# Cross-attention and expert feed-forward on one core: a written order for every stage, with the first feed-forward group prepared in the last attention units

## The chip, the cores and the metric

The kernel runs on one core of a Trainium2 chip. The metric is the device time of one execution in microseconds (us); lower is better. The time given for the kernel is the median of its runs. One execution is also recorded by the hardware profiler; all durations below come from that record. The engines are TensorE (PE, with its weight loads as PEld), VectorE (DVE), ScalarE (ACT), GpSimd (POOL) and SyncE (SP), which issues most of the DMAs.

## The reference

All data are float32. There are 32 sequences of 100 tokens, 512 features wide (3200 tokens), and a context of 722 rows for each, of which the causal mask leaves the first 100 visible.

```python
# attention, 16 heads of 32
q = layernorm(x) @ WQ.T;  k = ctx @ WK.T;  v = ctx @ WV.T
scores = einsum('bhqd,bhkd->bhqk', q, k) / sqrt(32)       # causal mask
y = einsum('bhqk,bhkd->bhqd', softmax(scores), v)
x = x + y @ Wfc.T + bfc
# feed-forward on h = layernorm(x): a shared expert and 16 routed ones, inner width 1024
shared = (gelu(h @ Ws_g.T) * (h @ Ws_u.T)) @ Ws_d.T       # all 3200 tokens
s = softmax(h @ gate_w.T)                                 # every token, 16 experts
w, idx = top_k(s, 12)                                     # 12 tokens of each sequence for each expert
eo = (gelu(h[idx] @ Wg.T) * (h[idx] @ Wu.T)) @ Wd.T * w   # 384 tokens per expert
x = x + shared + scatter_add(eo)
```

## The kernel before

Every float32 matrix product of a projection or of the feed-forward is made of three matmuls (`mm3`): each operand is split into a high half (a copy to fp32r on ACT) and a low half (the operand less its high half, on DVE or POOL), and high times high, high times low and low times high are added in PSUM.

**Attention** (`attention`) works in 32 units: a superblock `sb` of four sequences (400 tokens, `SB`) by a column block `c` of four heads. The K and V projections run over blocks of context rows (`KVB`: two blocks of 256 rows, then seven of 384); they go to DRAM and come back by unit (`kload`, `vload`). The first two blocks, the weights' splits and the first superblock of x are made in a prologue, whose order a scheduler chooses by a simulated timeline (`TCKW`). The units are in a list written by hand (`tc.manual_schedule()`): every engine, SP among them, takes its instructions in the written order. Unit `u` makes the q projection of `u` (`qproj`), scores and softmax of `u - 1`, and the transposed probabilities (`p_turn`, copied out of PSUM by `p_keep`) and products with V (`values`) of `u - 2`, so two further units drain the pipeline. The softmax is done in two halves: `sm_max` (DVE), `sm_sub` (POOL), `sm_exp` (ACT), `sm_sum` (DVE), `sm_mul` (POOL). From unit `KS` = 2 to unit 29 each unit makes one of four K projections of a block (`kproj`, kept by `kkeep`) and, in three of four units, one V projection (`vproj`). The x of the next superblock is normalised (`x_stats`, `x_norm` on DVE, the inverse root on POOL) and transposed on PE (`x_turn`), whose output shares two PSUM buffers, `ms`, with `p_turn` and `values`. In the unit, `x_norm` stands behind the second `sm_sum`:

```python
                if a is not None:
                    sm_sum(a, 1)
                    sm_mul(a, 1)
                if xs:
                    x_norm(sb + 1, c)
```

The result y of a unit goes to DRAM (`y_keep`, L291).

**Feed-forward** (`feed_forward`) has no written order. The scheduler places all its instructions, and its first ones among the last attention units. It loads and splits Wfc (L448 to L450, lower half on POOL), held back until the k load of unit `LATE` = 26 is issued (`issue_after`). The 25 tiles of 128 tokens form ten groups (`GROUPS`: five of two tiles, five of three). `prep` of a group loads y (`big<-yD`) and x, splits y, and for each tile makes y times Wfc on PE, adds bias and x, normalises, stores the normalised rows (`xnD`), transposes and splits them; then the router's logits. `ffn` runs over eight chunks of the inner width: 24 gate and up matmuls (`gu`) of as many columns as the group has tokens, gelu (ACT), product, split into `hh` and `hl`, and nine down matmuls (`dn`, for three tiles) one chunk later. Weights come as 768 KB chunks through two buffers (`wraw`) and are split by ACT (L435) and DVE (L436); the shared expert's chunks are split once and kept. `hook` prepares the next group after chunk 0; before the last group it also calls `route`, which takes the top 12 through DRAM and makes the slot lists. For each expert the rows are gathered by an indirect DMA on POOL, transposed, run through the same `ffn`, scaled, and added to the output by an indirect DMA (L610). While an expert runs, the scheduler splits the next expert's weights into the place of the chunks done.

Of the kernel before, what the change touches and what calls it, by code (L numbers as in the profile page):

```python
# [23 lines left out]
FB = dict(pre=2, r=7, raw=2, g=2, h=2)  # L24
# [3 lines left out]
KS = 2  # L28
LATE = 26
BUF = dict(cr=4, raw=5, cx=8, x=6, v=2, kk=2, kt=3, vt=2, q=3, p=5, pt=5, y=2, pj=2, sc=1, tr=2)  # L30
GROUPS = [2, 2, 2, 2, 2, 3, 3, 3, 3, 3]
# [28 lines left out]
def attention(tc, K):  # L60
    nc = tc.nc
    with ExitStack() as ctx:
        def pool(name, bufs, **kw):
            return ctx.enter_context(tc.tile_pool(name=name, bufs=bufs, **kw))

        xp = pool("a_x", BUF["x"])
        xnp = [pool("a_xn0", 1)]
        raw = pool("a_raw", BUF["raw"])
        crp = pool("a_cr", BUF["cr"])
        cxp = pool("a_cx", BUF["cx"])  # L70
        kkp = pool("a_kk", BUF["kk"])
        ktp = pool("a_kt", BUF["kt"])
        vtp = pool("a_vt", BUF["vt"])
        wpool = pool("a_w", 1)
        xnp.append(pool("a_xn1", 1))
        vp = pool("a_v", BUF["v"])
        qp = pool("a_q", BUF["q"])
        cst = pool("a_c", 1)
        stp = pool("a_st", 3)
        pp = pool("a_p", BUF["p"])  # L80
        ptp = pool("a_pt", BUF["pt"])
        yp = pool("a_y", BUF["y"])
        ps_kv = pool("a_kv", BUF["pj"], space=PSUM)
        ps_sc = pool("a_sc", BUF["sc"], space=PSUM)
# [5 lines left out]
        for w in range(3):  # L90
            WH.append(wpool.tile([128, NC4, D], FR, name=f"wh{w}"))
            WL.append(wpool.tile([128, NC4, D], FR, name=f"wl{w}"))
# [3 lines left out]
        def split(hi, lo, src):  # L96
            nc.scalar.copy(hi, src)
            nc.vector.tensor_tensor(lo, src, f32(hi), ALU.subtract)

        def load_w(w, dk):  # L100
            r = raw.tile([128, D], F32, name="raw")
            nc.sync.dma_start(r, K.wA[w, :, dk, :])
            split(WH[w][:, dk, :], WL[w][:, dk, :], r)

        def load_wc(w, c):
            r = raw.tile([128, D], F32, name="raw")
            rv = r.rearrange("p (d n) -> p d n", d=NC4)
            cs = slice(c * 128, (c + 1) * 128)
            nc.sync.dma_start(rv, K.wA[w, :, :, cs])
            split(WH[w][:, :, cs], WL[w][:, :, cs], rv)  # L110
# [43 lines left out]
        def x_turn(sb, b):  # L154
            xt = cur["x", sb, b]
            tp = ps_ms.tile([128, NC4, S], F32, name="ms")
            for dk in range(NC4):
                nc.tensor.transpose(tp[:, dk, :], xt[:, dk * 128:(dk + 1) * 128],  # L158
                                    K.ident[0:S, 0:S])
            cs = slice(b * S, (b + 1) * S)  # L160
            split(cur["xh", sb][:, :, cs], cur["xl", sb][:, :, cs], tp)
# [32 lines left out]
        def kload(u):  # L194
            sb, c = divmod(u, NC4)
            kt = ktp.tile([128, SB], F32, name="kt")
            cur["dma"] = nc.sync.dma_start(kt, K.kD[:, c, sb * SB:(sb + 1) * SB])
# [66 lines left out]
        def p_turn(u, b):  # L264
            p = cur["p", u, b // 2][0]
            tp = ps_ms.tile([128, NC4, S], F32, name="ms")
            for h in range(4):
                nc.tensor.transpose(tp[0:S, h, :], p[:, b % 2, h, :], K.ident[0:S, 0:S])  # L268
            cur["tp", u, b] = tp

        def p_keep(u, b):
            pt = ptp.tile([S, 4, S], F32, name="pt")
            nc.scalar.copy(pt, cur["tp", u, b][0:S])  # L273
            cur["pt", u, b] = pt

        def values(u):
            sb, c = divmod(u, NC4)
            ys = ps_ms.tile([128, NC4, S], F32, name="ms")
            for b in range(4):
                pt, v = cur["pt", u, b], cur["v", sb, b]  # L280
                for h in range(4):
                    d0 = c * 128 + 32 * h
                    nc.tensor.matmul(ys[32 * h:32 * h + 32, b, :], v[:, d0:d0 + 32],  # L283
# [3 lines left out]
        def y_keep(u):  # L287
            sb, c = divmod(u, NC4)
            y = yp.tile([128, SB], F32, name="y")
            nc.scalar.copy(y.rearrange("p (b s) -> p b s", b=4), cur["y", u])  # L290
            nc.sync.dma_start(K.yD[c, :, sb * SB:(sb + 1) * SB], y)  # L291

        nsb = K.nsb
        NU = nsb * NC4
        nc.gpsimd.dma_start(mask, K.mask)
        load_wc(0, 0)
        for d in range(NC4):
            ctx_load(0, d)
        for d in range(NC4):
            ctx_split(0, d, nc.vector)  # L300
        for c in range(1, NC4):
            load_wc(0, c)
        for dk in range(NC4):
            load_w(1, dk)
        for c in range(NC4):
            kkeep(0, c, kproj(0, c))
        for d in range(NC4):
            ctx_load(1, d)
        for d in range(NC4):
            ctx_split(1, d, nc.vector)  # L310
        for b in range(4):
            x_load(0, b)
            x_stats(0, b)
            x_norm(0, b)
        load_wc(2, 0)
        for i in range(KVB[0]):
            vkeep(0, i, vproj(0, i))
        for b in range(4):
            x_turn(0, b)
        for c in range(NC4):  # L320
            kkeep(1, c, kproj(1, c))
        for c in range(1, NC4):
            load_wc(2, c)
        for i in range(KVB[1]):
            vkeep(1, i, vproj(1, i))
        for d in range(2):
            ctx_load(2, d)
        for d in range(2):
            ctx_split(2, d)
        for d in range(2, NC4):  # L330
            ctx_load(2, d)
        x_load(1, 0)

        NU = nsb * NC4
        blocks = range(2, len(KVB))
        with tc.manual_schedule():
            for u in range(NU + 2):
                sb, c = divmod(u, NC4)
                mine, a, back = u < NU, u - 1, u - 2
                a = a if 0 <= a < NU else None  # L340
# [5 lines left out]
                jn, d = divmod(u + 2, NC4)  # L346
                jn += 2
                jl, dl = divmod(u + 4, NC4)
                jl += 2
                xs = mine and sb + 1 < nsb  # L350
                if mine:
# [391 lines left out]
```

## Time and profile before

| | |
|---|---|
| median of 3 runs | 1761.69 us (1761.47 to 1763.64) |
| profiled execution, its own time | 1757.8 us |
| its span, first to last instruction | 1756.0 us |
| mean granted clock of TensorE | 0.985 |
| busy: PE, DVE, ACT, POOL | 97%, 49%, 39%, 25% |
| DMA | 211.15 MB, mean 120 GB/s |

The busy shares are over the span. "Clock" is the share of TensorE's full clock that the chip granted. A line of a timeline gives start, duration, engine, source line, operation, output and input with their shapes, and in brackets how long the engine had stood before it and what released it. A line of the waits gives the waiting engine and line, what it waited for, and us in total, number of times and longest. Matmul records end by a model, so a busy PE is not always a PE at its peak.

### The profile page before, as it was taken

The numbers are of one execution on the slowest core, as the hardware profiler recorded it, in microseconds if no ns is written. First come the engines' busy times: TensorE is split into PE (matmuls) and PEld (weight loads), VectorE is DVE, ScalarE is ACT, GpSimd is POOL, SyncE is SP. The second block draws the span as 40 slices with busy tenths as digits, with TensorE's granted clock in tenths as the row PEclk, the third lists the DMA queues.
The fourth block names the chain that finished last, engine by engine and source line by source line (L and its number), as shares of the span: only waits on it lengthen the run. The fifth ranks groups of instructions, "written<-read, shape, count | busy, mean of one in ns | idle before, by whom it ended". The sixth has DMA issues, their size and how long they took to land.

```text
span 1756.0 us, 28445 instructions
## 1 busy us (share of the span) xinstructions
PE 1698.6 (97%) x11272; PEld 1560.4 (89%) x11272; DVE 854.9 (49%) x2131; ACT 685.8 (39%) x1100; POOL 440.8 (25%) x401
## 2 busy tenths in 40 slices
PE   7999999959999999999999999999999999999996
PEld 6888888848999999999989999999999999999996
DVE  5666666665334443333454444444444445444441
ACT  4455555544222221121243444444444444444431
POOL 2777777661100110011020111110111110011111
PEclk9999999979999999999999999999999999999998
DMA  7344444364111121101053555544555554454431
GB/s 234 102 130 130 137 131 132 119 206 137 55 55 58 64 66 43 37 31 49 28 193 134 161 162 157 149 141 147 162 162 150 156 160 134 156 155 136 142 90 18
DMA packets 83652, 211.15 MB, mean 120 GB/s; under 512 B 9569, under 2 KB 36434, under 8 KB 83520
## 3 DMA queue, kind: packets, MB, share of 16 engines
q1 hardware_dynamic: 72592, 184.07, 31.8%
q0 software_dynamic: 10784, 25.21, 7.4%
q8 instruction: 88, 1.44, 0.3%
q14 instruction: 44, 0.36, 0.1%
q10 hardware_dynamic: 144, 0.07, 0.0%
HBM read 163.71 MB, written 45.60 MB: 119 GB/s over the span
## 4 chain that ended last, share of the span: by engine, by line
PE 90%; DVE 2%; DMA 2%; ACT 2%; POOL 2%; issue 1%; SPq 0%; POOLq 0%; ACTq 0%; DVEq 0%
PE gu L55 46%; PE dn L55 23%; PE kv L55 10%; PE m L55 4%; PE ms L268 2%; PE sc L227 2%; PE ms L283 1%; PE m L595 1%; POOL p L247 1%; DVE p L238 1%; PE m L495 1%; PE ms L158 1%; PE m L504 1%; DMA r<-wA 0%; ACT p L251 0%
## 5 line engine op out<-in xcount | busy, mean ns | idle before, releaser
L55 PE MATMUL gu<-xh,whl 128*128 128x384 f32 (+1 forms) x3328 | 656.8, 327 | 0.1
L55 PEld LDWEIGHTS gu<-xh,whl 128*128 128x128 f32 x3328 | 561.8, 188 | 16.8 <-ACT g L542 0.3
L436 DVE TENSOR_TENSOR whl<-wraw,whl 128x1536 fp32r<-128x1536 f32 x136 | 240.8, 1771 | 279.6 <-ACT whl L435 277.7
L55 PE MATMUL dn<-whl,hh 128*128 128x512 f32 x1168 | 362.5, 395 | 0.0
L55 PE MATMUL gu<-xl,whl 128*128 128x384 f32 (+1 forms) x1664 | 345.3, 326 | 0.0
L55 PEld LDWEIGHTS gu<-xl,whl 128*128 128x128 f32 x1664 | 285.9, 188 | 2.3
L435 ACT CAST whl<-wraw 128x1536 fp32r<-128x1536 f32 x136 | 201.0, 1479 | 136.9 <-PE dn L55 128.2
L610 POOL DMA_INDIRECT out_dram<-r,isl x48 | 77.3, 1610 | 693.7 <-ACT r L609 683.9
L546 ACT CAST hh<-g 128x384 fp32r<-128x384 f32 (+1 forms) x208 | 102.4, 492 | 380.0 <-DVE g L543 379.0
L55 PEld LDWEIGHTS dn<-whl,hh 128*128 128x128 f32 x1168 | 214.3, 188 | 33.9
L55 PE MATMUL dn<-whl,hl 128*128 128x512 f32 x584 | 225.4, 395 | 0.0
L542 ACT ACTIVATE g<-gu 128x384 f32<-128x384 f32 (+1 forms) x208 | 97.8, 470 | 270.3 <-PE gu L55 251.3
L543 DVE TENSOR_TENSOR g<-g,gu 128x384 f32<-128x384 f32 (+1 forms) x208 | 109.4, 526 | 188.6 <-PE gu L55 187.5
L547 DVE TENSOR_TENSOR hl<-g,hh 128x384 fp32r<-128x384 f32 (+1 forms) x208 | 112.4, 540 | 102.6 <-ACT hh L546 102.6
L55 PEld LDWEIGHTS dn<-whl,hl 128*128 128x128 f32 x584 | 109.5, 188 | 25.5
L247 POOL TENSOR_TENSOR p<-p,mx 100x800 f32<-100x800 f32 x64 | 97.9, 1548 | 80.2 <-DVE mx L238 76.0
L238 DVE CUSTOM_DVE_ANT_0 p<-sc,mask 100x100 f32<-100x100 f32 x512 | 95.7, 257 | 22.7 <-PE sc L227 22.7
L262 POOL TENSOR_TENSOR p<-p,sm 100x800 f32<-100x800 f32 x64 | 101.9, 1593 | 8.0 <-DVE sm L257 7.0
L488 POOL TENSOR_SCALAR rs<-mv 128x1 f32<-128x1 f32 x25 | 6.9, 278 | 341.1 <-DVE mv L486 341.1
L256 DVE TENSOR_REDUCE sm<-p 100x8 f32<-100x800 f32 x64 | 63.1, 985 | 32.2 <-ACT p L251 32.2
L590 POOL DMA_INDIRECT big<-xnD,isl x48 | 51.3, 1069 | 95.7 <-DVE isl L673 61.3
L268 PE MATMUL ms<-ident,p 100*100 100x100 f32 x512 | 57.4, 257 | 11.4 <-ACT pt L273 7.8
(116 smaller groups left out, 1659.8 us busy)
## 6 DMA issues: line engine op xcount, KB each, us to landing
wraw<-wE SPq DMA_DIRECT2D x136, 768.0 KB
xt<-x SPq DMA_DIRECT2D x32, 200.0 KB
vD<-vt SPq DMA_DIRECT2D x25, 256.0 KB
kt<-kD SPq DMA_DIRECT2D x32, 200.0 KB
v<-vD SPq DMA_DIRECT2D x8, 800.0 KB
yD<-y SPq DMA_DIRECT2D x32, 200.0 KB
r<-x SPq DMA_DIRECT2D x25, 256.0 KB
xnD<-r SPq DMA_DIRECT2D x25, 256.0 KB
```

The source lines that it names most:

```text
L55: r = nc.tensor.matmul(out, t[0][a], t[1][b], start=(first and i == 0), stop=(last and i == n - 1))
L238: nc.vector.tensor_tensor_reduce(out=p[:, bb, h, :], in0=sc[:, h, cs], in1=mask, scale=ISCALE, scalar=NEG, op0=ALU.add, op1=ALU.max, accum ...
L247: nc.gpsimd.tensor_tensor(pv, pv, mx[:, :, None].to_broadcast([S, 8, S]), ALU.subtract)
L262: nc.gpsimd.tensor_tensor(pv, pv, sm[:, :, None].to_broadcast([S, 8, S]), ALU.mult)
L268: nc.tensor.transpose(tp[0:S, h, :], p[:, b % 2, h, :], K.ident[0:S, 0:S])
L435: nc.scalar.copy(h, r)
L436: nc.vector.tensor_tensor(l, r, f32(h), ALU.subtract)
L542: nc.scalar.activation(g[:, 0:n], pg[:, 0:n], AF.Gelu)
L543: nc.vector.tensor_tensor(g[:, 0:n], g[:, 0:n], pu[:, 0:n], ALU.mult)
L546: nc.scalar.copy(hh[:, 0:n], g[:, 0:n])
L547: nc.vector.tensor_tensor(hl[:, 0:n], g[:, 0:n], f32(hh[:, 0:n]), ALU.subtract)
L610: ins = nc.gpsimd.indirect_dma_start(out=K.out, out_offset=bass.IndirectOffsetOnAxis(ap=isl[:, i:i + 1], axis=0), in_=o, in_offset=None, c ...
```

## The change

All stages get a written order. For PE, ACT, DVE and SP it holds to the end; POOL keeps its written order in attention, and the scheduler places its instructions after that.

- The prologue is a list of steps (`prologue`), with loads apart from splits. The lower halves of three of the four WQ column blocks are made on POOL. `KS` is 1, so K and V projections run in units 1 to 28, and V of the second block moves partly into unit 0. `x_norm` moves ahead of the second `sm_sum`.
- Wfc is loaded and split in units 9 to 12 (`FC_AT`), lower half on DVE; the other constants follow in unit 13.
- The pools of the K and V path close after unit 28, and the feed-forward's buffers open in their place. The first group (now three tiles) is prepared in units 29 to 31 and the drain after them: y and x loads at the end of unit 28, bias, `split_y`, `fc` and so on between the attention steps (`end` is 0 in unit 29, -1 in unit 28); the first two weight chunks are loaded in unit 29 and split in thirds or whole. Gate and up of chunk 0 (`begin`) stand before the last unit's `p_turn`.
- The feed-forward is a class whose `job` runs eight chunks; after each chunk's gate, up and `hidden` come the steps listed in `mid[f]`, then the down products of the chunk before, then the steps listed in `post[f]`. Preparation of the next group, routing, gathers, `gturn` (transposes of gathered rows) and weight splits are placed by these lists.
- There are nine groups instead of ten. Attention's x buffers are 5 instead of 6, its raw buffers 6 instead of 5; transposed tiles in PSUM are laid out 128 apart instead of 100.

The core of the diff:

```diff
-KS = 2
-LATE = 26
-GROUPS = [2, 2, 2, 2, 2, 3, 3, 3, 3, 3]
+KS = 1
+FC_AT = 9
+GROUPS = [3, 2, 2, 3, 3, 3, 3, 3, 3]
...
+                if FC_AT <= u < FC_AT + NC4:
+                    fr = load_w(3, u - FC_AT)
+                if u == FC_AT + NC4:
+                    F.load_consts()
+                if end == 0:
+                    F.chunk_load()
+                    F.chunk_load()
+                if end == 1:
+                    pr.add(0)
+                    pr.stats(0)
+                    pr.rsqrt(0)
+                if end == 2:
+                    pr.add(2)
+                    pr.stats(2)
+                    pr.rsqrt(1)
+                    pr.store(0)
                 if a is not None:
                     scores(a)
...
                 if a is not None:
                     sm_exp(a, 0)
+                if end == 0:
+                    pr.split_y(0)
                 if back is not None:
                     p_turn(back, 0)
                     p_turn(back, 1)
                     p_keep(back, 0)
                     p_keep(back, 1)
...
+                if end == 1:
+                    pr.fc(1)
+                    pr.norm(0)
+                    F.chunk_split(0, 0)
+                if end == 2:
+                    pr.turn(0)
+                    pr.norm(2)
...
+                if xs:
+                    x_norm(sb + 1, c)
                 if a is not None:
                     sm_sum(a, 1)
                     sm_mul(a, 1)
-                if xs:
-                    x_norm(sb + 1, c)
...
+                if end == 0:
+                    pr.fc(0)
+                if end == 1:
+                    pr.fc(2)
+                if end == 2:
+                    F.chunk_split(0, 1)
+                    pr.turn(1)
                 if back is not None:
                     values(back)
+                if end == -1:
+                    kvctx.close()
+                    F.open_first()
...
+                    pr.load_y()
+                    for i in range(pr.nt):
+                        pr.load_x(i)
...
+    def job(self, e, xh, xl, nt, sink, mid, post):
+        acc = []
+        for f in range(NFC):
...
+                parts = self.gate_up(e * NFC + f, xh, xl, nt)
+            for p in mid.get(f, []):
+                p()
+            self.down()
+            self.pend = acc, f, nt, sink, parts
+            for p in post.get(f, []):
+                p()
...
+            if g == 0:
+                for f in range(NFC - 2):
+                    at(post, f, lambda f=f: self.chunk_split(f + 2))
+            if g + 1 < ng:
+                p = self.prep(g + 1)
+                at(post, 0, p.load_y, *[lambda i=i: p.load_x(i) for i in range(p.nt)])
+                at(post, 1, *[lambda i=i: p.bias(i) for i in range(p.nt)])
+                at(post, 1, p.split_y)
+                for i in range(p.nt):
+                    at(mid, 2 + i, lambda p=p, i=i: p.fc(i))
+                    at(post, 2 + i, lambda p=p, i=i: p.ln(i))
+                    at(post, 3 + i, lambda p=p, i=i: p.store(i))
+                    at(mid, 4 + i, lambda p=p, i=i: p.turn(i))
+                at(mid, 7, p.logits)
+                at(post, 7, p.tokens)
+            if g == ng - 1:
+                r = Route(self)
+                at(mid, 0, lambda: r.turn(0, 12))
+                at(mid, 1, lambda: r.turn(12, 12), lambda: r.turn(24, 1))
+                at(post, 1, r.load)
+                at(post, 2, *[lambda j=j: r.top(j) for j in range(4)], r.exchange)
+                at(mid, 4, r.slots)
+                at(post, 4, lambda: self.gather(0, r))
+                for i in range(NST):
+                    at(mid, 7, lambda i=i: self.gturn(0, i))
+                for f in range(1, NFC):
+                    at(post, f, lambda f=f: self.chunk_split(NFC + f - 1))
...
+            if g + 2 == ng:
+                Route.softmax(self)
...
+        for e in range(self.K.ne):
+            mid, post = {}, {}
+            if e + 1 < self.K.ne:
+                at(post, 0, lambda: self.gather(e + 1, r))
+                for i in range(NST):
+                    at(mid, 3 + i, lambda i=i: self.gturn(e + 1, i))
+                at(post, 0, lambda: self.chunk_split(NFC * (e + 2) - 1))
+                for f in range(1, NFC):
+                    at(post, f, lambda f=f: self.chunk_split(NFC * (e + 2) + f - 1))
```

Weight chunks still pass through two raw buffers: each finished split asks for the next load (`chunk_load`). After unit 31 the drain is written out in this order: scores and `sm_max` of the last unit, `p_turn` of the one before, `turn(2)`, `values`, the halves of the last softmax with the logits and the last third of chunk 0 between them, chunk 1's split, gate and up of chunk 0, `tokens`, then `p_turn`, `values` and `y_keep` of the last unit.

## The prediction

> **What bounds the kernel now.** I read the page first, then a table of windows cut where TensorE (PE) changes its behaviour, then the waits of PE, then the timeline at the waits.
>
> ```profile
> PE 1698.6 (97%) x11272; PEld 1560.4 (89%) x11272; DVE 854.9 (49%) x2131; ACT 685.8 (39%) x1100; POOL 440.8 (25%) x401
> ...
> PEclk9999999979999999999999999999999999999998
> ```
>
> PE is busy for 97% of 1756.0 us, so no other engine bounds the whole; what can be won is the 57 us in which PE stands, and whatever it works at a reduced clock. The windows (columns: PE, PEld, DVE, ACT, POOL busy us with instruction counts, clock, DMA share, GB/s) say where:
>
> ```profile
> 0.00:45.00 45.00, 34.40 (x220) 30.04 (x220) 24.50 (x77) 21.58 (x45) 12.77 (x22) 1.00 0.75 233
> 45.00:60.00 15.00, 12.97 (x100) 11.74 (x104) 8.82 (x43) 5.88 (x13) 11.99 (x11) 0.77 0.12 42
> 60.00:345.00 285.00, 274.94 (x3142) 248.76 (x3137) 188.99 (x1071) 153.63 (x311) 204.79 (x181) 0.98 0.43 129
> 345.00:400.00 55.00, 36.65 (x408) 30.63 (x407) 33.60 (x128) 28.19 (x46) 35.24 (x25) 0.78 0.60 194
> 400.00:900.00 500.00, 499.64 (x2931) 455.59 (x2930) 208.81 (x379) 113.30 (x210) 55.10 (x74) 1.00 0.19 62
> 900.00:925.00 25.00, 22.73 (x129) 20.57 (x128) 14.87 (x18) 11.00 (x16) 4.12 (x4) 1.00 0.60 209
> 925.00:1742.20 817.20, 817.20 (x4359) 763.10 (x4357) 375.26 (x418) 351.53 (x464) 112.55 (x85) 1.00 0.48 141
> 1742.20:1756.00 13.80, 0.01 (x1) 0.00 (x0) 0.00 (x0) 0.72 (x2) 4.27 (x3) 0.62 0.47 57
> ```
>
> The feed-forward stage (400 to 1742) has no idle PE but 2.3 us at 900 to 925. The losses lie in attention and at its end (345 to 400: 18.3 us idle). PE's own waits name them:
>
> ```profile
> PE ms L158 <- DVE xt L152: 15.4, 7, 5.3
> PE ms L268 <- ACT pt L273: 7.8, 1, 7.8
> ```
>
> The first is seven waits of `x_turn` for `x_norm`: one of 5.3 us at 41.7, where units 0 and 1 have no K and V projection, and six of 1.68 us, one in each unit with no V projection. There DVE does `sm_sum` first and the norm after it (normed at 90.07, PE turns at 90.71):
>
> ```profile
> 88.93 0.99 DVE L256 TENSOR_REDUCE sm<-p 100x8 f32<-100x800 f32 x1 [0.32 <-ACT p L251]
> 89.95 0.20 DVE L257 RECIPROCAL sm<-sm 100x8 f32<-100x8 f32 x1
> 90.07 0.50 DVE L152 TENSOR_SCALAR xt<-xt,mv,rs 100x512 f32<-100x512 f32 x1
> ```
>
> The 7.8 us wait is an ACT copy behind the Wfc conversion, whose load comes late:
>
> ```profile
> 356.06 1.29 ACT L449 CAST wfh<-r 128x512 fp32r<-128x512 f32 x2 [6.95 <-DMA r<-wA]
> ```
>
> The clock costs more. Two pairs of windows, each with a wait for `x_norm` in its first:
>
> ```profile
> 130.94:134.35 3.41, 1.73 (x50) 1.32 (x51) 2.07 (x4) 2.23 (x7) 3.39 (x3) 1.00 0.44 112
> 134.35:137.77 3.42, 3.42 (x39) 3.22 (x32) 2.28 (x24) 0.36 (x1) 1.12 (x2) 0.50 0.89 232
> ...
> 260.62:264.03 3.41, 1.96 (x64) 1.72 (x68) 1.84 (x4) 2.19 (x6) 3.39 (x3) 1.00 0.49 139
> 264.03:267.50 3.47, 3.47 (x38) 3.32 (x31) 3.11 (x33) 0.49 (x1) 1.65 (x2) 1.00 0.88 227
> ```
>
> With 1.73 us busy of 3.41 the next 3.42 us run at half clock; with 1.96 they do not. This happens at 134, 220 and 305. The Trainium skill ("TensorE: Matmul & The Clock Gate", section "Why this matters for your kernels") has the clock fall after one whole idle window, and allows gaps up to about 3 us. By it the 1.68 us gaps cost only themselves and the change wins nothing on the clock here (a sum of -23.7 below, 1738); by the rows each half-clock window costs 3.41/2 = 1.7 us more, three times 5.1 us (-28.8, 1733). The measured rows decide, and I follow them.
>
> **The change part by part** (minus is a gain, in us of PE's path, against the profiled 1756.0 span and its 1757.8 run).
>
> 1. *Start of the units* (KS 2 to 1). Unit 1 now has a K projection (12 x 0.174 = 2.1) and a V projection (12 x 0.234 = 2.8) between its q projection and `x_turn`: 4.9 us of work, plus the earlier norm, against the 5.3 us wait. It goes, and with it the half clock behind it (0.77 in 45 to 60: 5.4 us busy at half clock, 2.7 lost): -8.0. The work is not lost: it leaves the end, see 3.
>
> 2. *`x_norm` ahead of the second `sm_sum`*. The norm can run after `rs` (POOL done at 88.77): 0.5 us, to 89.3. What is late next is the PSUM buffer that `p_keep` frees, about 89.6: some 0.65 us stay of 1.68. Six times: -6.2. The second `sm_sum` ends 0.4 us later, hidden, since POOL is in the first `sm_mul` until 90.35. A gap of 0.65 leaves over 2.6 busy of 3.41, so the three half-clock windows go: -5.1. Bounds: 0 and -15.2.
>
> 3. *End of attention, 345 to 400 and the first feed-forward group*. Now: 18.3 idle, 0.3 at 416, and half clock over 18 us busy (5.9, 3.4, 8.6 in three stretches), 9.0: 27.6. The four Wfc loads move to units 9 to 12 (ACT 0.63, DVE 0.68 each in place of POOL 1.28; DVE is free for a third of 60 to 345: hidden). I went through units 28 to 31 and the rest by hand, each queue in written order, with the rows' durations: scores 0.9, q 2.2, four `p_turn` 1.4, values 0.85; 16 `sm_max` 2.95, `sm_sum` 1.2, exp 0.88, POOL's `sm_sub` 1.52, `sm_mul` 1.55, bias 1.27. Unit 28: 0.7 idle as now. Unit 29: PE has 8.2 of work with fc(0); ACT stands at `split_y` for the y block, `p_keep` behind it: 1.9 idle. Unit 30: PE 11.0, DVE 10.3: none. Unit 31: PE only 6.2. DVE first does add and statistics of block 2 (1.5), so `sm_max` ends at 5.9 after the scores' start, POOL's first `sm_sub` at 6.0, ACT's exp at 6.9, and the two `p_keep` behind it at 7.3 and 7.7; PE is through its first `p_turn` at 3.8 and `turn(0)` wants the buffer of 7.4: 3.6 idle. The fourth `p_turn` waits for the buffer of `turn(0)`, whose lower half stands on DVE behind `norm(1)` and `sm_sum`: 1.8 more. Drain: values, logits and chunk 0's gate and up (4.2) cover most of the last softmax: 1.7. Half clock after the 3.6: 2.0, at least 0, at most 5. Sum 11.7: -15.9. On SP, y (0.77 MB), three x (0.77), k and two weight chunks (1.5) now stand ahead of `vload(7)` (0.8): 4.1 MB at some 200 GB/s land after 20 us, just when values(28) wants them. I take 0; up to +3.
>
> 4. *Groups* 2x5+3x5 to 2x2+3x7. A chunk's 24 gate/up matmuls take 2.86 us with 256 columns and 4.19 with 384: 114.4+167.6 becomes 45.8+234.6: -1.6.
>
> 5. *Prologue in written order*. The loads that gate PE are the same until V's first weights; small waits of 2.4 become about 2.0 (four `x_turn` in a row wait 1.2 for buffers): -0.4, from -2 to +4.
>
> 6. *Shared groups in written order*. `load_y` goes out after the previous group's outputs, about 3.4 us after the chunk-0 matmuls end; it was issued chunks ahead. How long it takes:
>
> ```profile
> 594.51 0.37 SPq L463 DMA_DIRECT2D big<-yD  x1
> ...
> 599.96 1.28 POOL L477 TENSOR_TENSOR r<-r,bfc 128x512 f32<-128x512 f32 x1 [3.22 <-DMA r<-x]
> ```
>
> So 5.5 us, with an x load behind it. yh follows by 1.5 (L467), at 11; fc(0) comes at 12.6 with three tiles and needs yl only eight matmuls later: no wait. Group 0 loads weights ahead of y (+2.4), group 2 has two tiles (+1.4): +4, from 0 to +9. The output stores, x loads and `store` behind it on SP have a chunk or more.
>
> 7. *Routing in written order*. In the last group `turn` stands ahead of the previous group's last down products. LG needs reduce, subtract, exp with a table load (1.28), reduce, multiply, 4.4 us, against 4.2 of cover: 0.7, then 1.9 for a PSUM buffer behind `hidden`; second `turn` 1.7; `slots` 1.0 behind two small DMAs; the three `gturn` in one chunk 1.4. Sum 6.7 in place of 2.3: +4.4, from -2 to +9.
>
> 8. *Experts*. ACT per 6.28 us chunk: gelu 0.49, hh 0.52, weights 1.48; the ACT copy already waits for `dn` now (at 1013.19, 0.92), and PE has no gap. `gturn` (0.4 PE) is now in chunks 3 to 5; in the changed order of instructions POOL's gathers precede older scatters, but each waits for a buffer free before those scatters have data. 0, covered by about 2 us of slack between hl and its down products. The 13.8 us tail stays.
>
> Sum: -8.0-6.2-5.1-15.9-1.6-0.4+4.0+4.4 = -28.8. The span becomes 1727. The profiled run lies 3.9 below the median 1761.7; on the median: 1733.
>
> **Rivals.** (a) *Written order is free after attention*: parts 6 and 7 cost nothing and unit 31 half: -41, 1721. For it: 400 to 900 has DVE at 42%. Chance 0.17. (b) *The softmax chain keeps the tail*: POOL and DVE bound units 29 to 31 more than I counted, v is late, and 3 brings 3 only: -16, 1746. For it: POOL busy 35 of 55 us. Chance 0.13. (c) *The clock and `x_turn` waits stay*, since the buffer of `p_keep` and not the norm was last: 2 brings nothing, -17.5, 1744. Against: the norm ends 0.14 ahead of PE's start, `p_keep` a whole copy earlier. Chance 0.06. (d) *Slower: y blocks come late in every group.* fc stands ahead of the down products in PE's queue, ACT's gelu behind `split_y`. From a load of 7 us on (1.6 of slack) each of eight preparations pays; to outdo -28.8 by over 3.5 it must pay 4.5 each, a load of 12: 1769. Against: 62 GB/s in 400 to 900. Chance 0.03. (e) The gains hold but new waits eat them all, within 0.2% (3.5 us, about what a measurement of this kernel tells from no change): 0.01.
>
> **Numbers.** My case 0.60: 1733, its own costs 1724 to 1742. The range takes in (a), (b) and (c): 1716 to 1750. Faster 0.95, same 0.01, slower 0.04.
>
> **What would show it.** Right: no wait of `x_turn` at the first units; waits of 0.6 to 0.7 in units without V; clock 1.00 from 60 to 300; attention's units ending some 20 us earlier with 8 to 10 us idle in the last three, most at `turn(0)`; a few us idle at the routing. Wrong: waits of `m` for `yh` in most groups, or any wait that repeats per chunk in the experts.

## The result, and the profile after

The changed kernel takes 1750.18 us (median of 4 runs, 1748.54 to 1750.64); the kernel before, on the same chip in the same session, 1761.58 (4 runs, 1760.12 to 1763.64). The ratio is 0.9933, 95% interval 0.9916 to 0.995: a gain of 11.4 us where 28.8 was forecast. The profiled execution of the changed kernel is the slowest of its runs (span 1748.8), and that of the kernel before is faster than all four of the runs above (span 1756.0). So the two traces differ by 7.2 us only, and the sums below are made against 7.2.

The page of the changed kernel: busy time of each engine, and the granted clock.

```profile
PE 1698.7 (97%) x11072; PEld 1559.6 (89%) x11072; DVE 885.7 (51%) x2118; ACT 681.2 (39%) x1086; POOL 445.0 (25%) x399
...
PEclk9999999989999999999999999999999999999998
```

DVE is busy 31 us longer than before (854.9) with 13 instructions fewer: some of its instructions have become slower. Other groups of DVE went up and down and nearly cancel; what stays is the norm, before and after (count | busy us, mean ns of one | idle before, releaser):

```profile
L152 DVE TENSOR_SCALAR xt<-xt,mv,rs 100x512 f32<-100x512 f32 x32 | 16.1, 506 | 1.5 <-POOL rs L146 1.5
```

```profile
L161 DVE TENSOR_SCALAR xt<-xt,mv,rs 100x512 f32<-100x512 f32 x32 | 47.6, 1490 | 13.1 <-POOL rs L155 13.0
```

The table of windows by stage (columns as before: length, PE, PEld, DVE, ACT, POOL, clock, DMA share, GB/s):

```profile
0.00:40.77 40.77, 31.84 (x177) 27.70 (x177) 17.61 (x37) 19.41 (x42) 13.63 (x22) 0.96 0.71 215
40.77:337.18 296.41, 284.83 (x3187) 257.95 (x3187) 231.04 (x1119) 160.16 (x322) 211.29 (x189) 0.98 0.43 133
337.18:398.37 61.19, 51.36 (x553) 44.08 (x550) 43.82 (x175) 31.88 (x57) 34.90 (x26) 0.87 0.46 151
398.37:850.72 452.35, 451.01 (x2470) 409.47 (x2470) 173.41 (x289) 94.69 (x172) 58.93 (x66) 1.00 0.17 59
850.72:905.85 55.13, 50.40 (x275) 45.57 (x274) 32.44 (x72) 17.77 (x24) 8.07 (x7) 1.00 0.43 138
905.85:1735.15 829.30, 829.30 (x4419) 774.83 (x4418) 387.36 (x427) 356.56 (x470) 113.93 (x88) 1.00 0.50 143
```

These are the prologue, the units up to the last K projection, the end of attention up to the first down product, the shared groups, the routing and the experts. Length less PE busy is idle time: 8.9, 11.6, 9.8, 1.3, 4.7 and 0. PE's waits say what for:

```profile
PE ms L167 <- DVE xt L161: 10.4, 7, 1.7
PE kv L55 <- ACT cxh L134: 5.1, 1, 5.1
PE ms L277 <- ACT pt L282: 4.1, 3, 2.3
PE ms L885 <- ACT pt L282: 3.7, 1, 3.7
PE m L938 <- DVE big L940: 3.1, 2, 1.6
PE kv L55 <- ACT kk L200: 3.0, 2, 2.2
```

The first line is `x_turn` waiting for `x_norm`. Of the wait of 5.3 us at the first units 0.45 is left, but the six waits in units without V are as long as before, 1.64 to 1.68. At one of them the timeline shows why:

```profile
121.00 0.57 POOL L155 TENSOR_TENSOR rs<-rs,nhalf 100x1 f32<-100x1 f32 x1
...
121.56 1.52 POOL L271 TENSOR_TENSOR p<-p,sm 100x800 f32<-100x800 f32 x1
...
121.60 1.76 DVE L161 TENSOR_SCALAR xt<-xt,mv,rs 100x512 f32<-100x512 f32 x1 [0.19 <-POOL rs L155]
...
123.50 0.53 PE L167 MATMUL ms<-ident,xt 100*128 100x100 f32 x4 [1.68 <-DVE xt L161]
```

The norm does start earlier, at 121.60, right after `rs`, as the new order has it. But POOL's `sm_mul` has started 0.04 us before, and the norm, which took 0.50 in its old place, takes 1.76 and ends 0.28 after `sm_mul`. In all, 25 of the 32 norms take 1743 to 1823 ns. Of the other seven, the first five take 542 to 547, and two that started 0.23 ahead of an `sm_mul` take 496 and 498.

### The profile page after: what moved, and what is told of

Its sections match the earlier page's. It is cut to its first block, busy times and chain, and to the rows that moved or that the text cites. A ratio compares the mean times of both kernels' runs of the same rounds, so it can differ in the third digit from the quotient of the medians.

```text
span 1748.8 us, 27994 instructions
## 1 busy us (share of the span) xinstructions
PE 1698.7 (97%) x11072; PEld 1559.6 (89%) x11072; DVE 885.7 (51%) x2118; ACT 681.2 (39%) x1086; POOL 445.0 (25%) x399
## 4 chain that ended last, share of the span: by engine, by line
PE 91%; DVE 3%; DMA 2%; POOL 2%; ACT 1%; issue 1%; SPq 0%; POOLq 0%; ACTq 0%; DVEq 0%
PE gu L55 46%; PE dn L55 23%; PE kv L55 10%; PE m L55 3%; PE ms L277 2%; PE sc L236 2%; PE ms L292 1%; POOL p L256 1%; DMA big<-yD 1%; PE m L779 1%; DVE p L247 1%; PE ms L167 1%; DVE xt L161 1%; DMA kD<-kk 1%; PE m L894 1%
## 5 line engine op out<-in xcount | busy, mean ns | idle before, releaser
L55 PE MATMUL gu<-xh,whl 128*128 128x384 f32 (+1 forms) x3200 | 645.0, 333 | 1.3 <-ACT g L654 1.3
L55 PE MATMUL dn<-whl,hh 128*128 128x512 f32 x1168 | 372.4, 400 | 0.0
L627 DVE TENSOR_TENSOR whl<-wraw,whl 128x1536 fp32r<-128x1536 f32 (+1 forms) x138 | 242.1, 1755 | 241.9 <-ACT whl L626 241.8
L55 PE MATMUL gu<-xl,whl 128*128 128x384 f32 (+1 forms) x1600 | 338.1, 333 | 0.0
L55 PEld LDWEIGHTS gu<-xl,whl 128*128 128x128 f32 x1600 | 280.8, 188 | 0.0
L626 ACT CAST whl<-wraw 128x1536 fp32r<-128x1536 f32 (+1 forms) x138 | 201.4, 1460 | 105.3 <-PE dn L55 103.4
L55 PE MATMUL dn<-whl,hl 128*128 128x512 f32 x584 | 230.9, 395 | 0.0
L793 POOL DMA_INDIRECT out_dram<-x,isl x48 | 77.5, 1615 | 365.5 <-ACT x L792 355.8
L837 POOL TENSOR_TENSOR x<-x,bfc 128x512 f32<-128x512 f32 x24 | 44.4, 1875 | 248.4 <-DMA x<-x 248.4
L260 ACT ACTIVATE p<-p 100x800 f32<-100x800 f32 x64 | 56.2, 879 | 17.3 <-POOL p L256 17.3
```

What stands on the lines that cost most here:

```text
L55: r = nc.tensor.matmul(out, t[0][a], t[1][b], start=(first and i == 0), stop=(last and i == n - 1))
L626: nc.scalar.copy(h[:, cs], r[:, cs])
L627: nc.vector.tensor_tensor(l[:, cs], r[:, cs], f32(h[:, cs]), ALU.subtract)
L793: ins = nc.gpsimd.indirect_dma_start(out=self.K.out, out_offset=bass.IndirectOffsetOnAxis(ap=r.isl[:, i:i + 1], axis=0), in_=o, in_offset= ...
```

## The experiments

Two theories of the missing part. **P**, the prediction's step 2: the norm takes 0.5 us, and its place in the order decides. **T**: in the new place it runs beside POOL's `sm_mul` and cannot finish before it. A rival **B**: the buffer that `p_keep` frees was last all along. In the table, the ratio to the kernel before of the same session, and from the trace the idle PE time with the half-clock loss (busy time in windows of clock 0.50, halved) in prologue, units and end of attention, in us. The changed kernel was timed in one session and the experiments in others, in which the kernel before took 1759.2 to 1759.7 and not 1761.6; so the ratios compare better than the times.

| kernel | time | ratio, 95% | prologue | units | end |
|---|---|---|---|---|---|
| before (its profiled run) | 1761.58 | 1 | 7.3+0 | 15.4+7.8 | 18.4+8.9 |
| changed | 1750.18 | 0.9933 (0.9916-0.995) | 8.9+1.7 | 11.6+6.8 | 9.8+7.2 |
| e1 norm back | 1749.53 | 0.9943 (0.9929-0.9956) | 9.5+3.1 | 11.2+5.1 | 10.8+4.1 |
| e2 norm ahead of first sum | 1745.97 | 0.9922 (0.991-0.9934) | 9.5+1.5 | 10.2+0 | 10.7+7.5 |
| e3 norm in the first sm_max | 1748.00 | 0.9931 (0.9919-0.9943) | 9.6+1.7 | 8.5+1.7 | 11.0+4.7 |
| e4 fills | 1744.49 | 0.9913 (0.9899-0.9928) | 10.5+2.5 | 4.5+0 | 7.4+1.7 |
| e5 three kk buffers | 1745.48 | 0.9915 (0.99-0.993) | 6.7+0 | 11.7+6.8 | 9.7+7.2 |
| e6 p_keep ahead of exp | 1749.00 | 0.9942 (0.9929-0.9956) | 9.5+1.7 | 11.6+6.8 | 11.2+3.4 |
| e7 gate weights later | 1748.49 | 0.9939 (0.9924-0.9954) | 9.6+1.7 | 12.1+5.1 | 10.8+4.3 |
| e8 together | 1737.80 | 0.9879 (0.9864-0.9894) | 7.4+0 | 5.7+0 | 9.8+4.4 |
| e9 unit 31 in a further order | 1746.75 | 0.9931 (0.9917-0.9945) | 9.2+1.7 | 12.8+5.1 | 7.8+3.0 |
| e10 together, further | 1730.89 | 0.9836 (0.9822-0.9849) | 6.8+0 | 4.6+0 | 8.8+3.3 |
| e11 before, norm moved alone | 1760.61 | 1.0001 (0.9993-1.001) | 7.4+0 | 15.4+8.3 | 19.8+12.5 |
| e12 before, norm ahead of first sum | 1752.39 | 0.9962 (0.9949-0.9976) | 8.6+0 | 9.7+3.3 | 21.3+8.8 |

**e1: the norm back in its old place**, in the changed kernel.

```diff
-                if xs:
-                    x_norm(sb + 1, c)
                 if a is not None:
                     sm_sum(a, 1)
                     sm_mul(a, 1)
+                if xs:
+                    x_norm(sb + 1, c)
```

> The changed kernel with x_norm put back behind the second sm_sum/sm_mul; all else as changed. Theory P (the prediction's step 2: the norm takes 0.5 us wherever it stands, so its place in the order decides): the six waits of x_turn in units without V, which would have to be 0.65 in the changed kernel, become 1.7, and the time grows by 6 to 11 us. Theory T (in the new place the norm starts together with POOL's sm_mul, is held until that ends and takes 1.76 us instead of 0.5, so that it ends where it ended before): the waits are 1.6 to 1.7 in both kernels, the norm takes 0.5 again, and the time stays within 2.5 us of the changed kernel's 1750.2.

Theory T holds: the six waits are 1.64 to 1.68 and the time is not longer. The timeline of the same unit:

```profile
121.22 3.19 POOL L271 TENSOR_TENSOR p<-p,sm 100x800 f32<-100x800 f32 x2
121.40 0.99 DVE L265 TENSOR_REDUCE sm<-p 100x8 f32<-100x800 f32 x1 [0.32 <-ACT p L260]
...
122.54 0.49 DVE L161 TENSOR_SCALAR xt<-xt,mv,rs 100x512 f32<-100x512 f32 x1
...
123.18 0.53 PE L167 MATMUL ms<-ident,xt 100*128 100x100 f32 x4 [1.67 <-DVE xt L161]
```

Behind the sum the norm comes as the first `sm_mul` ends, and takes 0.49. `sm_sum` itself, a TENSOR_REDUCE, takes 0.99 beside POOL and 0.97 to 0.99 alone: not every DVE operation is affected. From old place or new, the norm is done 0.28 to 0.29 after the end of the first `sm_mul`, and so PE's wait is the same.

**e11 and e12: the same part of the change alone, in the kernel before** (e11: the two lines moved as in the change; e12: to the place of e2, next).

> The kernel before with one part of the change alone: x_norm ahead of the second sm_sum/sm_mul. The prediction's step 2 forecast -11.3 us for this part. Theory T (held by POOL's sm_mul from its start to its end): the norm takes 1.75 us, x_turn's six waits stay at 1.6 to 1.7 and the time is that of before within 2.5 us.

> The kernel before with x_norm ahead of the first sm_sum, and nothing else. Theory T: the norm takes 0.55 us, the six waits fall to about 0.65, the three half-clock windows between 60 and 310 go, and 4 to 11 us are won against before. If the gain seen with this place in the changed kernel came from something else of that kernel: within 2.5 us of before.

The group of the norm in e11, then in e12 (count | busy us, mean ns of one | idle before, releaser):

```profile
L152 DVE TENSOR_SCALAR xt<-xt,mv,rs 100x512 f32<-100x512 f32 x32 | 46.2, 1448 | 6.5 <-POOL rs L146 6.3
```

```profile
L152 DVE TENSOR_SCALAR xt<-xt,mv,rs 100x512 f32<-100x512 f32 x32 | 17.4, 545 | 54.7 <-POOL rs L146 54.7
```

e11 is the clearest of the runs: the move that was to bring 11.3 us brings nothing (1.0001, 0.9993 to 1.001), with the six waits at 1.66 to 1.68. One place further up it brings 0.38% (6.7 us): the waits are 0.67 to 0.68, the three half-clock windows are gone, and idle time and half clock of the units' stage fall from 23.2 us to 13.0. (In this one trace prologue and end lose 4.1 us more than in that of the kernel before.) So step 2's aim was sound, also its figure for what stays (0.65), and the place was wrong.

**e2: the norm ahead of the first sum**, in the changed kernel.

```diff
                     sm_exp(a, 1)
+                if xs:
+                    x_norm(sb + 1, c)
+                if a is not None:
                     sm_sum(a, 0)
                     sm_mul(a, 0)
```

(and the old call removed)

> The changed kernel with x_norm one place further up, ahead of the first sm_sum: there POOL has no large operation until the first sum is done. Theory T: the norm takes 0.55 us, x_turn's six waits of 1.67 fall to 0.5 to 0.7 (the buffer that p_keep frees is then last), most of the four half-clock windows go; the first sm_mul comes some 0.7 us later, which may give back up to 3 us. Time -4 to -13 us against 1750.2. Rival B (the buffer of p_keep was last all along): waits stay at 1.6 to 1.7, time within 2 us. Rival D (the later first sm_mul becomes the new bound): waits of p_turn for p in every unit, slower than 1750.2.

```profile
119.94 0.55 DVE L161 TENSOR_SCALAR xt<-xt,mv,rs 100x512 f32<-100x512 f32 x1 [1.75 <-POOL rs L155]
...
120.84 0.56 PE L167 MATMUL ms<-ident,xt 100*128 100x100 f32 x4 [0.67 <-ACT pt L282]
...
121.76 1.52 POOL L271 TENSOR_TENSOR p<-p,sm 100x800 f32<-100x800 f32 x1 [1.86 <-DVE sm L266]
```

The norm takes 0.55, `x_turn` now waits for `p_keep`'s copy, as B would have it, but only for 0.64 to 0.97: B is right as the next bound, wrong as the present one. No half-clock window is left in the units, whose stage is 5.1 us shorter (291.3 against 296.4). The price is in the last line: the first `sm_mul` comes after the norm, and new waits of 0.4 to 0.8 for `p_keep` appear in single units. The time is 4.2 us below the changed kernel's, but the intervals of the two ratios overlap, so e12 is the better evidence for the gain.

**e3: statistics one unit ahead, the norm inside the first `sm_max`**, where POOL has nothing that is large.

```diff
-                    sm_max(a, 0)
+                    sm_max(a, 0, 7 if xs else None, lambda: x_norm(sb + 1, c))
...
-                    sn, bn = divmod(u + 5, NC4)
+                    sn, bn = divmod(u + 6, NC4)
```

> The changed kernel with statistics and 1/sqrt one unit ahead (x loads too) and x_norm between the seventh and eighth operation of the first sm_max, a unit part before x_turn wants it. Theory T: the norm takes 0.55 us in units where POOL is free at that place, up to 1.5 elsewhere, and is never last for x_turn; the six waits fall to 0.4 to 0.7, the half-clock windows between 60 and 340 go: -8 to -14 us against 1750.2, and at least as good as putting it ahead of the first sm_sum. Rival B (buffer of p_keep last): waits stay at 1.6 to 1.7, time within 2 us.

The norm takes 0.54 and is never last, but the waits are 0.97 and not 0.4 to 0.7: ACT makes `kkeep`'s copy (0.48) ahead of the `p_keep` that frees the buffer. The units' stage is 4.0 us shorter; the time is not clearly better than the changed kernel's. Waits and time both miss their ranges. e8 puts `kkeep` behind.

**e4: dummy matmuls in the idle time**: 6 of 128x512 ahead of `x_turn` in the units without V, 13 ahead of `turn(0)` in unit 31.

```diff
+                    if kv and not vv:
+                        fill(6)
                     x_turn(sb + 1, c)
...
+                    fill(13)
                     pr.turn(0)
```

> The changed kernel with dummy matmuls (their result is not used) where PE waits: 6 of 128x512 ahead of x_turn in the units without V, 13 ahead of turn(0) of the first group in unit 31. They take the idle time and nothing else. If the half-clock windows come from the idle time (prediction's steps 2 and 3): the four of 3.4 us between 60 and 340 go (-6.8 us) and the one of 13.7 us at 368 shrinks or goes (up to -6.9): -5 to -13 us against 1750.2. If the half clock has another cause: windows stay where they are, time +0 to +3 us.

Work was added and the time fell: no half-clock window is left from 45 to 340, and of the 13.7 us at 368 none; one of 3.4 stays at 344. The ratio is 0.9913 (0.9899 to 0.9928), clear of e1's 0.9943 (0.9929 to 0.9956) in the same session, and just overlapping that of the changed kernel. The windows of the changed kernel at the wait that ends at 165.53, and the stage of the units of e4:

```profile
163.70:167.10 3.40, 1.74 (x50) 1.33 (x52) 3.37 (x5) 2.60 (x7) 1.84 (x2) 1.00 0.57 173
167.10:170.50 3.40, 3.40 (x39) 3.20 (x32) 0.47 (x1) 0.00 (x0) 2.58 (x3) 0.50 0.54 154
```

```profile
42.30:334.30 292.00, 287.46 (x3223) 258.48 (x3223) 233.71 (x1119) 159.80 (x322) 211.06 (x189) 1.00 0.44 135
```

1.74 us busy of 3.40, then a window at 0.50, as the prediction read it in the kernel before. Its price can be had from runs in which the units' code is alike: PE is busy 284.8 to 284.9 us there with four windows (changed, e5, e6) and 283.1 to 283.5 with three (e1, e7, e9): 1.3 to 1.8 for one, against the 1.7 of the prediction. How many of the six equal waits are followed by such a window, three or four, changes from trace to trace.

**e5: three `kk` buffers instead of two** (`BUF`: `kk=2` to `kk=3`).

> The changed kernel with three kk buffers instead of two, so that in the prologue the third K copy need not wait for the store of the first, which stands on SP behind 12 loads. If that wait is what holds PE at 13.5 (2.2 to 4.4 us in the runs so far) and at 20.5 (0 to 0.7): the first shrinks by at least 1.5 us, the fourth copy may wait instead; -1 to -4 us. If PE waits there for the weights of V from HBM: nothing changes, within 1.5 us.

The prologue was to gain 0.4 us and loses 3.3. In the changed kernel's trace:

```profile
9.45 0.59 SPq L201 DMA_DIRECT2D kD<-kk  x1
...
15.66 0.37 ACT L200 COPY kk<-kv 128x256 f32<-128x256 f32 x1 [2.50 <-DMA kD<-kk]
...
16.08 0.50 PE L55 MATMUL kv<-wh,cxh 128*128 128x512 f32 x1 [2.24 <-ACT kk L200]
```

The third K copy waits 2.50 for a buffer, that is for the store shown: SP issued it at 9.45, behind the loads written ahead of it, and it landed 6.1 us later. With a third buffer 0.22 is left of PE's waits for `kk`, the half-clock window at 17 is gone, and the prologue loses 6.7 us instead of 10.6. The ratio is 0.9915; its interval still overlaps that of the changed kernel, so the gain is read from the trace.

**e6, e9: the order in units 29 and 31.** e6 puts `p_keep` of the first two blocks ahead of the first exp; e9 also puts `turn(0)` right behind them and `add(2)`, `stats(2)` behind `sm_max`.

```diff
+                if end in (0, 2):
+                    for b in range(2):
+                        p_turn(back, b)
+                        p_keep(back, b)
+                if end == 2:                     # e9 only
+                    pr.turn(0)
+                    pr.norm(1)
                 if a is not None:
                     sm_exp(a, 0)
+                if end == 2:                     # e9 only
+                    pr.add(2)
+                    pr.stats(2)
+                    pr.rsqrt(2)
```

> The changed kernel with p_keep of the first two blocks ahead of the first exp (and of split_y) on ACT in units 29 and 31. The prediction's step 3 (turn(0) waits 3.6 us because the buffer's copy stands behind exp, and exp behind POOL and DVE): the wait of 3.7 at turn(0) falls to under 1, that of 2.2 in unit 29 to under 1, and the half-clock window behind turn(0) goes or shortens by 3.4 us or more: -5 to -9 us against 1750.2. Rival (the softmax chain of DVE and POOL bounds these units, the prediction's rival b): the idle time moves to the p_turn of the second half or to scores, and the gain is under 2 us.

The wait in unit 29 falls from 2.3 to 0.4; that in unit 31 moves, and grows from 3.7 to 4.5:

```profile
371.68 0.57 ACT L890 CAST xh<-ms 128x512 fp32r<-128x512 f32 x1
372.14 0.49 ACT L282 COPY pt<-ms 100x400 f32<-100x400 f32 x1
...
372.69 0.91 PE L277 MATMUL ms<-ident,p 100*100 100x100 f32 x4 [4.53 <-ACT pt L282]
```

`turn(0)` is done at 367.8, but its ACT copy (L890) stands behind both exps, and PE's next `p_turn` behind that. The gain of -5 to -9 failed to come. The rival took the softmax chain for the bound; e9 tells whether it is that or the order.

> The changed kernel with units 29 and 31 in a further order: p_keep of the first two blocks ahead of exp in both; in unit 31 turn(0) right behind them (its ACT copy ahead of exp, its DVE subtract ahead of sm_sum), norm(1) before it counts, and add and statistics of block 2 behind sm_max instead of ahead of it. With p_keep alone ahead, the idle time only moved from turn(0) to the second pair of p_turn (4.5 us), whose buffer the subtract of turn(0) frees, behind norm(1) and sm_sum(0). If the order of the side work on ACT and DVE is what holds PE there, the two waits of unit 31 sum to under 2 us, the half-clock window of 6.8 us or more behind them goes, attention's end comes 4 to 7 us earlier, and the time is -4 to -8 us against 1750.2. If the softmax chain itself (DVE 3 us, POOL 3, ACT 1.8) is the bound, the idle time moves on to the last unit's softmax and under 2 us is won.

```profile
367.77 0.58 ACT L890 CAST xh<-ms 128x512 fp32r<-128x512 f32 x1 [0.35 <-PE ms L889]
...
369.14 0.55 PE L277 MATMUL ms<-ident,p 100*100 100x100 f32 x4 [1.05 <-DVE xl L891]
...
370.44 0.90 PE L889 MATMUL ms<-ident,xn 128*128 128x128 f32 x3 [0.76 <-ACT pt L282]
```

With the copy at 367.77 the two waits sum to 1.8, under the 2 expected, and the end of attention takes 56.0 us (61.2 in the changed kernel, 59.4 to 61.1 in e1, e5, e6 and e7): the order held PE, not the chain. But the half-clock window of 6.8 stays, and of the 3.5 to 5 us the times show little (ratio 0.9931): its gain is read from the trace alone.

**e7: the gate weights' conversion one unit behind their load.** The changed kernel has a wait that neither the kernel before nor the prediction had: a PE gap of 1.17 that ends at 175.7.

```profile
170.73 0.24 ACT L568 CAST gw<-gr 128x64 fp32r<-128x64 f32 x1 [4.14 <-DMA gr<-gwT]
```

In written order ACT comes to this copy in the same unit that issues the load.

> The changed kernel with the gate weights' conversion (memset, ACT copy, DVE subtract) one unit behind their load. The load is issued in unit 13 and the ACT copy of the same unit stands 4.1 us for it at 170.7, the DVE subtract behind it 3.4 us, and p_turn's buffer comes late: if so the PE gap of 1.2 us at 174 goes, -1 to -2 us. If the gap has another cause it stays.

```profile
191.79 0.24 ACT L573 CAST gw<-gr 128x64 fp32r<-128x64 f32 x1 [4.14 <-POOL gw L572]
```

A miss: the memset that clears the tile had moved along, POOL came to it behind its split of the context, and the same copy waits as long for POOL. The PE gap moved with the copy: none is left at 175, and one of 1.64 ends at 198.1. e10 leaves the memset with the load; the copy doesn't wait there, and PE does not stand from 168 to 200 (one PE gap of 0.94 stays at 166; the DVE half of the Wfc split, 1.35 beside POOL in that unit, may be its cause, which was not tried).

**e8 and e10: together.** e8 is e3, `kkeep` behind `p_keep`, e5, e6 and e7. e10 adds e9's order and the memset, and spreads the routing's turns (at most two PSUM tiles for each chunk, everything behind them a chunk later).

> All of it together: statistics a unit ahead with x_norm inside the first sm_max, in units without V the K copy behind the p_keep pair (x_turn's wait was 0.97 with the K copy ahead), three kk buffers, gate weights converted a unit later, p_keep ahead of exp in units 29 and 31. If the losses are the ones named so far and add up: x_turn waits 0.5, no half clock from 45 to 340, one such window or none in 340 to 400; -12 to -18 us against 1750.2, that is 1732 to 1738.

> The kernel with everything together (1737.8) plus three edits: that order of unit 31; the memset of the gate weights' tile with its load in unit 13, the ACT copy and subtract in unit 14 (with the memset in unit 14 too ACT waited 4.1 us for POOL); and the routing's turns spread over chunks 0 to 2 of the last group with two PSUM tiles each instead of three and four, everything behind them one chunk later. Expected: no PE gap of 0.9 to 1.6 at 167 and 190 (-1 to -2), unit 31 as above (-3 to -6), routing's idle 4.7 falls to 1.6 to 2 (the three gturn in one chunk stay) unless the gather now comes late (+1 to +5). Sum 1727 to 1734.

e8 is 1737.80, at the end of its range: the units lose 5.7 us where the changed kernel loses 18.4, and no window at half clock is left there. e10 is 1730.89, 0.9836 (0.9822 to 0.9849) of before: routing loses 1.6 where the changed kernel loses 4.7, the end of attention 12.1 (changed kernel 17.0, e8 14.2). This version beats both kernels.

## Why the prediction was wrong

It said 1733 with a range of 1716 to 1750, and the result is 1750.18. What came true of its rivals is the effect of (c), "the clock and `x_turn` waits stay" (1744, chance 0.06), but not its reason: the norm was still last, and not the buffer of `p_keep`. The result is 6 us above that rival's figure too, so further steps failed. Step by step, forecast against what the two traces show (idle time and half clock, against the traces' 7.2):

| step | forecast | measured |
|---|---|---|
| 1 start of the units | -8.0 | -7.6 |
| 2 `x_norm` ahead of the second sum | -11.3 | +2.8 |
| 3 end of attention | -15.9 | -10.4 |
| 4, 8 groups, experts | -1.6 | +0.8 |
| 5 prologue | -0.4 | +3.3 |
| 6 shared groups | +4.0 | +1.5 |
| 7 routing | +4.4 | +2.5 |
| end | 0 | -0.1 |
| sum | -28.8 | -7.2 |

**Step 1** was right in both terms: the wait went, and the half clock behind it.

**Step 2** is the step that failed: "0.5 us, to 89.3". The duration was taken from a norm that started 0.2 us before the end of an `sm_mul`, and was carried to a place where it starts beside the beginning of one. The six waits did not change; a fourth of them met a half-clock window (+1.7), and the gap behind the gate weights' copy added 1.2. The page that speaks against the move is the Trainium skill's "SBUF — State Buffer", section "Who interferes with whom": GpSimd's only SBUF port pair is the second pair of VectorE, one of the two holds it for its whole instruction; tensor_scalar can come under this, and so can operations with two SBUF inputs beside a GpSimd instruction that reads SBUF; tensor_reduce never does. The runs agree: 1756 ns (median of 25) against 542 to 547 alone, and 0.97 to 0.99 for the TENSOR_REDUCE either way. The single records also tell that the norm stood still and did not run slowly. In the kernel before, 27 norms start 0.20 to 0.27 us before the end of an `sm_mul`, and end 0.28 to 0.30 after it; in the changed kernel, 24 start 1.46 to 1.48 before that end, and end 0.28 to 0.29 after it. More than a microsecond of additional time beside POOL brought the norm no further. So the 0.50 that the prediction started from was itself the row of a norm that waited for POOL. The small subtract of the gate weights shows the same. It takes 0.23 with POOL idle (changed kernel, at 171.01), and in e10, where it comes up as the second of two `sm_mul` begins, 1.50 for the same 64 elements, to 0.08 after `sm_mul`'s end:

```profile
179.30 3.01 POOL L273 TENSOR_TENSOR p<-p,sm 100x800 f32<-100x800 f32 x2 [0.28 <-ACT p L262]
...
180.89 1.50 DVE L587 TENSOR_TENSOR gw<-gr,gw 128x64 fp32r<-128x64 f32 x1 [0.49 <-ACT gw L586]
```

By this rule step 2 comes to 0 and the forecast to 1744. The trace of the kernel before had the sign of it as well, in the feed-forward's norm, once beside POOL's bias and once without:

```profile
449.91 1.29 POOL L477 TENSOR_TENSOR r<-r,bfc 128x512 f32<-128x512 f32 x1
449.98 1.50 DVE L491 TENSOR_SCALAR r<-r,mv,rs 128x512 f32<-128x512 f32 x1 [0.99 <-POOL rs L489]
...
460.85 0.55 DVE L491 TENSOR_SCALAR r<-r,mv,rs 128x512 f32<-128x512 f32 x1 [0.46 <-POOL rs L489]
```

Twelve of its 25 take 0.54 to 0.55, thirteen 1.50 to 1.52.

**Step 3** was right in the idle time (9.8 for 9.7, the wait at `turn(0)` 3.69 for 3.6), in its sum with some luck: the fourth `p_turn` waits 0.64 where 1.8 was forecast, and small waits elsewhere make up for it. It was wrong in one term: half clock "2.0, at least 0, at most 5" is 7.2. The wait of 3.69 left 1.0 us busy of 3.5 and was followed not by one window but by 13.7 us at 0.50, in which further waits fell (5.9 us lost); a window at 395.8 makes the other 1.3. With the same order in this stage the term was 4.1 in e1 and 4.3 in e7, 7.2 in e5: it differs from trace to trace.

**Step 5** counted loads and not the `kk` stores behind them on SP: two waits of PE, 3.0 us, and a half-clock window, 1.7. The first of two waits was longer still in other runs (up to 4.4 in e4).

**Steps 6 and 7** were read rightly in kind (waits for `yh`, PSUM buffers behind DVE's copies, `gturn` in one chunk) and too high by 2.5 and 1.9. **Steps 4 and 8** get what is left when the others are taken off, +0.8 for -1.6. An expert takes 51.69 us for 51.60, 16 times, and its down matmuls follow each other in 236.7 ns in the mean instead of 233.0; no run looked for the reason.

The misses of 2, 3 and 5 make 23.3 us; 6 and 7 give 4.4 back, and the rest makes 2.7 more. What separates the 7.2 of the traces from the 11.4 of the medians is the runs in which the profiles were taken.

## What to carry to other kernels

A duration belongs to the place it was measured in: before an instruction is moved, look at what the other engine runs at its new place, and take the row in which the two run side by side; on VectorE next to GpSimd it can be three times the row without. In a written order, every wait of one instruction on ACT or SP is a wait of all behind it, so a load and its conversion, or a buffer's copy and the work that is not needed for it, want a unit between them. Where short idle times recur, a part of their price is the clock after them: filling them with useless matmuls (e4) shows in one run how much that is.

## What the runs showed of the hardware that was not expected

- An exclusive wait between VectorE and GpSimd: VectorE's fp32 TENSOR_SCALAR of 100x512 takes 542 to 547 ns alone and 1743 to 1823 when it starts with or just after a GpSimd TENSOR_TENSOR of 1.52 us (25 of 32 in the changed kernel). Wherever it starts beside that instruction, it ends 0.28 to 0.30 us after it. TENSOR_REDUCE, BATCH_NORM_STATS2 (0.69 beside POOL and alone) and an operation that reads PSUM (`xnl`, 0.57 in both cases) do not change. A subtract of 128x64 with both inputs in SBUF grew from 0.23 us to 1.50.
- One idle time of 1.64 to 1.68 us can cost a whole further window at half clock. In the changed kernel the four windows of 3.4 us with 1.74, 1.76, 1.82 and 1.90 us busy were each followed by one. The prediction's two rows (1.73 and 1.96) are no sharp limit, though: a window with 1.78 in e1 (at 77.8) and one with 1.74 in e7 (at 207.9) were not followed by one, and one with 1.99 in e9 (at 366.4) was. What decides between these is open. The six equal waits met three such windows in some traces and four in others, and the end of attention, in the changed kernel, e1, e2, e3, e5 and e7 with one and the same order there, lost 4.1 to 7.5 us at half clock. Whether one program varies as much is not shown, since each has one trace.
- Dummy matmuls in idle time made the kernel faster: 1744.49 (e4), against 1749.53 for e1 in the same session and 1750.18 for the changed kernel.
